# Graph layer on one core: edge lists loaded in runs of seven tiles, cast between the layer-norm groups

## The chip, the cores and the metric

The kernel runs on one core of a Trainium2 chip. A core has a matrix engine (TensorE, PE in the profile; PEld is its weight load), a vector engine (VectorE, DVE), a scalar engine (ScalarE, ACT), GpSimd (POOL) and a synchronisation engine (SyncE, SP) that here only issues DMAs. ACT and POOL issue DMAs as well. Every engine works through its own instructions in order, and waits on semaphores for the others. DMAs issued by SP, ACT and POOL go into separate queues (q1, q10 and q0 in the profile) which are served by the same 16 DMA engines. The metric is the time of one execution on the device in microseconds, less is better; the time before is a median of three runs.

## The reference

One graph layer over 6250 nodes of 256 features and 100000 edges, all in float32:

```
xn = layernorm(x)                                     # per node
x  = x + gnn(xn, src, dst) + mix(xn)
x  = x + lstm(layernorm(x))

gnn: neigh = segment_sum(xn[src], dst, N)             # dst is sorted
     h = relu(((1 + eps) * xn + neigh) @ W1 + b1) @ W2 + b2
     h = batchnorm over the nodes(h) * gamma + beta
mix: linear attention of 8 heads over all nodes, then an MLP with gelu, plus xn
lstm: one LSTM over the 6250 nodes in sequence, 256 wide, then two weighted running sums
```

`src` and `dst` are int32. The host pads both to 782 tiles of 128 edges (src with 0, dst with N = 6250) and hands them over as one flat run.

## The kernel before

**Layout.** The nodes lie as 125 rows ("c") by 50 steps ("s"), node = 50 c + s, with c on the partitions: `xn` is a tile of [125 of 128, 50, 256], and a DMA of n steps moves for each partition one run of n x 1024 bytes. `move` (L130) cuts every such DMA into two, partitions 0 to 111 and 112 to 124. `xnT` is the same transposed (features on the partitions), kept in the memory of `xr`.

**The head.** Six groups of steps (`LN_GROUPS`: 10, 10, 10, 10, 5, 5) are loaded by SP (L229), so twelve DMAs. Behind them on SP stand six small loads of `dst` in rows of 1024 edges (L230 to L235, tile `dg`), whose minima and maxima per 512 edges DVE takes at L317; at L329 it takes the same of runs of 256 edges for the first 34 groups. Those six go into `late`, the last ten steps of `xr`. ACT issues the load of a small table `vec` (L106) and then those of the edge lists themselves: src and dst each as 6 x 128 rows of 512 bytes (one row is one tile of 128 edges) and one DMA of the last 14 rows (L219, L220), into a corner of the tile `counts`. A tile of edges must end up as a column, an edge on each partition, because the gathers and selections of the later loop read columns. So L245 to L255 cast both lists to float32 on ACT (also in `late`), transpose 128 x 128 blocks on PE and copy them from PSUM to `si` (the sources as int32) and `drel` (the targets as float32).

The order on PE, DVE and ACT is written out by hand (`manual_schedule`); SP and POOL are ordered by the framework. Written order on these three: first the casts and transposes of both lists; then for each group `moments_of` (L270: statistics on DVE, one square root on ACT), in between DVE's operations the pending work of the group before (five small DVE operations and `normalise`, L287: scales two fifths of the rows on ACT, three fifths on POOL, and then issues the two writes of these steps to `xn_d` in DRAM on SP), then `columns_until` (L260): transposes of normalised steps on PE and copies to `xnT` on ACT, one group behind. After the last group come its normalisation, the reductions over `dg` and `flat`, and the remaining columns (L331), since these overwrite `late`. Then the loads of weights follow on SP: `w_qkv` into `m1` (L333), g1, g2, and the layer-norm table, w1 and w2 into `m2` (L336 to L339).

**Semaphores of DMAs.** The DMAs of SP and ACT share eight completion semaphores, given out in turn. A DMA that gets one that was used before waits on its issuing engine until that earlier DMA has landed. In the trace the order of handing out is `vec`, the first x load, the four edge loads, the other eleven x loads, the six `dg` loads, the twelve writes of `xn_d`, the weights.

**The rest.** Every gather (L372, POOL) fetches 128 rows of `xn_d` by a column of `si`, and can begin when all of `xn_d` is written. In a loop over 162 groups of four tiles, PE multiplies the rows by selections made from `drel` (L393) and DVE adds the result to `sums` (L403); the attention, the MLP, the counts of the first 34 groups and the node MLP (L574, L585) are interleaved with that by slots. The LSTM follows (L1042 to L1207), and a last pass adds and stores (L1288 to L1297).

Of the kernel before, what the change touches and what calls it, by code (L numbers as in the profile page):

```python
# [14 lines left out]
F32 = mybir.dt.float32  # L15
I32 = mybir.dt.int32
BF16 = mybir.dt.bfloat16
AF = mybir.ActivationFunctionType
# [5 lines left out]
P = 128  # L24
N, D, E = 6250, 256, 100000


NC, NS = 125, 50
HEADS, HC = 8, 32
KD = D // P  # L30
NE = -(-E // P)


GT, W = 4, 96
GROUPS = -(-NE // GT)
GE = GT * P
# [30 lines left out]
LN_GROUPS = [(0, 10), (10, 10), (20, 10), (30, 10), (40, 5), (45, 5)]  # L67
BANK = 512
# [22 lines left out]
def gps_layer(ctx: ExitStack, tc: tile.TileContext, x, src, dst, cols, rows, kvln, wqkv, mw1, mw2, gw1, gw2,  # L91
              wih, whh, blstm, out):
    nc = tc.nc
# [7 lines left out]
    ident = big.tile([P, P], F32, name="ident")  # L101
    make_identity(nc, ident)
    ones = big.tile([P, P], F32, name="ones")
# [34 lines left out]
    xr = big.tile([P, NS, D], F32, name="xr", tag="B")  # L138
    xnT = xr[:, :, :KD * NC].rearrange("p s (k c) -> p s k c", k=KD)

    m1 = big.tile([P, 2 * BANK * KD], F32, name="m1", tag="M1")
    w_qkv = m1[:, :KD * 3 * D].rearrange("p (k m) -> p k m", k=KD)
    kv_bias = m1[:, KD * 3 * D:]
    m2 = big.tile([P, 2 * BANK * KD], F32, name="m2", tag="M2")
# [11 lines left out]
    with ExitStack() as s1:  # L156
        wp = s1.enter_context(tc.tile_pool(name="wp", bufs=1))


        def edges_flat(t, start, ap):  # L160
            return bass.AP(tensor=t.tensor, offset=t.offset + start, ap=ap)

        si = wp.tile([P, NE], I32, name="si")
        base_i = wp.tile([1, GROUPS], I32, name="base_i")
        drel = wp.tile([P, NE], F32, name="drel")
        within = wp.tile([1, 1], I32, name="within")
        c_base = wp.tile([1, PAIRS], I32, name="c_base")
        g1 = wp.tile([P, KD, 2 * D], F32, name="g1")
# [6 lines left out]
        ope = wp.tile([P, 1], F32, name="ope")  # L175
# [14 lines left out]
        behind = place_x[:, at_x:]  # L190
# [13 lines left out]
        def from_bases(to, of, base_b, op):  # L204

            whole = NE // GT
            nc.vector.tensor_tensor(to[:, :whole * GT].rearrange("p (g t) -> p g t", t=GT),
                                    of[:, :whole * GT].rearrange("p (g t) -> p g t", t=GT),
                                    base_b[:, :whole, None].to_broadcast([P, whole, GT]), op=op)
            nc.vector.tensor_tensor(to[:, whole * GT:], of[:, whole * GT:],  # L210
                                    base_b[:, whole:].to_broadcast([P, NE - whole * GT]), op=op)

        with tc.tile_pool(name="ln1", bufs=2) as lp, tc.tile_pool(name="ps0", bufs=6, space=PSUM) as ps:
            FULL = NE // P
            late = xr.rearrange("p s d -> p (s d)")[:, (NS - 10) * D:]
            tiled = []
            for i, t in enumerate((src, dst)):
                s = behind[:, i * (FULL + 1) * P:(i + 1) * (FULL + 1) * P].bitcast(I32).rearrange("p (b e) -> p b e", e=P)
                nc.scalar.dma_start(s[:, :FULL, :], edges_flat(t, 0, [[P, P], [P * P, FULL], [1, P]]))  # L219
                nc.scalar.dma_start(s[:NE % P, FULL, :], edges_flat(t, FULL * P * P, [[P, NE % P], [1, P]]))  # L220
                tiled.append(s)

            rows_g = GROUPS // 2
            real = E - (rows_g - 1) * 2 * GE
            last = E - (GROUPS - 1) * GE
            flat = late[:, :2 * GE].bitcast(I32)
            dg = flat.rearrange("p (j e) -> p j e", j=2)
            for s0, n in LN_GROUPS:
                move(nc.sync, xn[:, s0:s0 + n, :], by_step(x)[:, s0:s0 + n, :])  # L229
# [3 lines left out]
            for at in range(real, 2 * GE, last):  # L233
                n = min(last, 2 * GE - at)
# [6 lines left out]
            nc.gpsimd.memset(counts, 0.0)  # L241

            with tc.manual_schedule(engines={mybir.EngineType.PE, mybir.EngineType.DVE, mybir.EngineType.Activation}):

                for s, to in zip(tiled, (si, drel)):  # L245
                    f = late[:, 2 * GE:2 * GE + (FULL + 1) * P].rearrange("p (b e) -> p b e", e=P)
                    nc.scalar.copy(f[:, :FULL, :], s[:, :FULL, :])
                    nc.scalar.copy(f[:NE % P, FULL, :], s[:NE % P, FULL, :])
                    for b0 in range(0, FULL + 1, 4):
                        pt = ps.tile([P, BANK], F32, name="mm")  # L250
                        w = min(NE - b0 * P, BANK)
                        for b in range(b0, min(b0 + 4, FULL + 1)):
                            r = min(P, NE - b * P)
                            nc.tensor.transpose(pt[:, (b - b0) * P:(b - b0) * P + r], f[:r, b, :], ident[:r, :r])
                        nc.scalar.copy(to[:, b0 * P:b0 * P + w], pt[:, :w])  # L255


                chunks = list(CHUNKS)
# [1 line left out]
                def columns_until(end):  # L260
                    while chunks and sum(chunks[0]) <= end:
                        s0, n = chunks.pop(0)
                        for k in range(KD):
                            pt = ps.tile([P, BANK], F32, name="mm")
                            for i in range(n):
                                nc.tensor.transpose(pt[:, i * NC:(i + 1) * NC], xn[:NC, s0 + i, k * P:(k + 1) * P],
                                                    ident[:NC, :NC])
                            nc.scalar.copy(xnT[:, s0:s0 + n, k, :], pt[:, :n * NC].rearrange("p (s c) -> p s c", c=NC))
# [33 lines left out]
                            partial(nc.vector.tensor_mul, rs, r, s), normalise]  # L302

                beside, done = [], 0
                for s0, n in LN_GROUPS:
                    more = moments_of(s0, n, beside)
                    while beside:
                        beside.pop(0)()
                    columns_until(done)
                    beside, done = more, s0  # L310
                for work in beside:
                    work()


                rows_c, each = COUNTED // 2, 2 * GT // CT
# [5 lines left out]
                for j in range(2):  # L321
                    b = ends[:rows_g, 0, j:j + 1]
                    pb = ps.tile([P, BANK], F32, name="mm")
                    nc.tensor.transpose(pb[:, :rows_g], b.to_broadcast([rows_g, P]), ident[:rows_g, :rows_g])
                    nc.vector.tensor_copy(base_b.rearrange("p (q j) -> p q j", j=2)[:, :, j], pb[:, :rows_g])
                    nc.vector.tensor_copy(base_i.rearrange("p (q j) -> p q j", j=2)[:, :, j], pb[:1, :rows_g])
                from_bases(drel, drel, base_b, ALU.subtract)
                for i, op in enumerate((ALU.min, ALU.max)):
                    nc.vector.tensor_reduce(pairs[:rows_c, i, :], flat[:rows_c, :].rearrange("p (j e) -> p j e", j=each),  # L329
# [31 lines left out]
        to = [sums[:, k, :N].rearrange("p (c s) -> p s c", s=NS) for k in range(KD)]  # L361
# [472 lines left out]
        with tc.If(held < GROUPS + PAIRS):  # L834
# [12 lines left out]
            base_b = mix_p.tile([P, 2 * D], F32, name="base_b", tag="t", bufs=4)  # L847
            nc.vector.tensor_copy(base_b[:, :GROUPS], pm[:, :GROUPS])
            from_bases(drel, drel, base_b[:, :GROUPS], ALU.add)
            with tc.For_i(0, NE, 1) as c:  # L850
                at = edge_p.tile([P, 1], I32, name="at1")
                nc.vector.tensor_copy(at, si[:, ds(c, 1)])
                d = edge_p.tile([P, 1], F32, name="d1")
                nc.vector.tensor_copy(d, drel[:, ds(c, 1)])
                g = gather(at[:, :1])
                for n0 in range(0, N + W, W):
                    w = min(W, N + W - n0)
# [14 lines left out]
        late = LATE / NS  # L872
# [71 lines left out]
    def summed(s, pool, pl):  # L944

        w = pool.tile([P, KD, NC], F32, name="w")
        nc.vector.scalar_tensor_tensor(w, pl[:, None, :].to_broadcast([P, KD, NC]), thr, of_step(s), op0=ALU.is_gt,
                                       op1=ALU.mult)
        if s == 0:
            nc.vector.tensor_copy(inc, w)  # L950
        else:
            nc.vector.tensor_add(inc, inc, w)
        for k in range(KD):
            weighted(s, 2, inc, k)
        return w
# [20 lines left out]
    with tc.tile_pool(name="lstm", bufs=2) as rp:  # L976
# [117 lines left out]
        with tc.manual_schedule(engines={mybir.EngineType.PE, mybir.EngineType.DVE, mybir.EngineType.Activation}):  # L1094
# [16 lines left out]
            for k in range(KD):  # L1111
                d = wl.tile([P, 1], F32, name="wlin_d")
# [57 lines left out]
        with tc.manual_schedule(engines={mybir.EngineType.PE, mybir.EngineType.DVE, mybir.EngineType.Activation}):  # L1170
            t = fetched.pop(0)
# [4 lines left out]
            w = None  # L1176
            for s in range(KEPT, NS):
                more = s + 1 < NS
                t = fetched.pop(0) if more else None
# [27 lines left out]
                w = summed(s - 1, rp, pl)  # L1207
# [9 lines left out]
        for i, (end, begin) in enumerate(((h, begin_h), (c, begin_c))):  # L1217
            d = rp.tile([P, KD, NC], F32, name="d", tag="h_w")[:, :, :NC - 1]
# [66 lines left out]
    with tc.tile_pool(name="post", bufs=3) as pp, tc.tile_pool(name="ps4", bufs=6, space=PSUM) as ps:  # L1285
        for i, (s0, n) in enumerate(CHUNKS):
# [4 lines left out]
            for s in range(s0, s0 + n):  # L1291
                pt = ps.tile([P, D], F32, name="pt")
# [66 lines left out]
```

## Time and profile before

| | |
|---|---|
| median of 3 runs (lowest, highest) | 1691.46 us (1687.46, 1699.31) |
| the profiled execution, its span | 1705.72 us, 1703.9 us |
| busy PE, DVE, ACT, POOL over the span | 86%, 55%, 39%, 41% |
| first gather | 62.97 us |
| products of the gathered rows (L393) | 70.1 to 1055.3 us |
| LSTM (L1042 to L1167) | 1077.8 to 1651.2 us |
| last pass (L1294) | from 1668.6 us |

The head in stretches of 5 us, from the table by stretches (busy us and, in brackets, instructions of each engine; then granted TensorE clock, mean busy share of the 16 DMA engines, and what they moved):

```profile
core 0: us, PE busy (x) PEld busy (x) DVE busy (x) ACT busy (x) POOL busy (x), PEclk, DMA share, GB/s
5.00:10.00 5.00, 0.00 (x0) 0.00 (x0) 1.14 (x6) 1.28 (x1) 5.00 (x1) 1.00 1.05 242
10.00:15.00 5.00, 0.00 (x0) 0.00 (x0) 3.14 (x18) 0.73 (x1) 0.48 (x2) 1.00 1.17 242
20.00:25.00 5.00, 0.00 (x0) 0.00 (x0) 0.00 (x0) 0.00 (x0) 0.00 (x0) 1.00 1.00 232
25.00:27.00 2.00, 0.00 (x0) 0.00 (x0) 0.00 (x0) 0.58 (x1) 0.00 (x0) 1.00 0.10 24
37.00:42.00 5.00, 3.76 (x17) 3.01 (x16) 4.96 (x29) 3.64 (x9) 3.26 (x6) 1.00 0.78 254
52.00:57.00 5.00, 2.55 (x23) 2.12 (x22) 4.49 (x14) 5.00 (x12) 2.54 (x5) 1.00 1.01 286
```

Up to 25 us the DMA engines are full while the four compute engines are nearly idle; from 25 to 27 us the DMA engines stand still too. From 37 us DVE has no idle time and paces the writes of `xn_d`.

### The profile page before, as it was taken

What the parts mean: (1) busy time and instruction counts of PE and PEld (TensorE: products, weight loads), DVE (VectorE), ACT (ScalarE), POOL (GpSimd) and SP (SyncE); (2) the same over time, 40 slices, a digit from 0 to 9 for tenths busy, and PEclk for the clock granted to TensorE, in tenths of its full rate; (3) what the DMA queues carried; (4) which work ended last, traced back from release to release, by engine and by line L of the source; (5) the groups of instructions that cost most, each with busy time, mean ns of one, the idle gap of its engine ahead of it and who ended that gap; (6) DMA issues with size and microseconds to landing.
All of it is one profiled execution on the core that took longest, in us unless ns stands there. A gap on an engine that the chain in (4) does not pass through costs nothing. (4 is left out here: it accounts for less than half of the span.)

```text
span 1703.9 us, 30469 instructions
## 1 busy us (share of the span) xinstructions
PE 1463.6 (86%) x11064; PEld 1383.9 (81%) x11064; DVE 938.7 (55%) x2931; ACT 659.7 (39%) x1921; POOL 694.1 (41%) x745
## 2 busy tenths in 40 slices
PE   2578888898888888988888888799999999999975
PEld 2567778787778888887888878799999999888874
DVE  3777677777773122212221222566667655788887
ACT  3532333333330122222222222566666643566650
POOL 3566666666666666666566663000010000000005
PEclk9789989999997999999999999899999999999997
DMA  8733323232334344433333333211111100233314
GB/s 212 232 85 89 89 86 88 84 89 84 89 88 137 116 128 130 125 107 101 92 102 102 102 99 106 86 62 74 62 74 67 68 38 2 73 110 109 110 50 152
DMA packets 64955, 165.98 MB, mean 97 GB/s; under 512 B 14409, under 2 KB 29499, under 8 KB 63792
## 3 DMA queue, kind: packets, MB, share of 16 engines
q0 software_dynamic: 31008, 84.71, 17.5%
q1 hardware_dynamic: 32016, 78.37, 14.3%
q8 instruction: 91, 1.49, 0.4%
q10 hardware_dynamic: 1768, 0.81, 0.2%
q14 instruction: 72, 0.59, 0.1%
HBM read 130.56 MB, written 33.28 MB: 96 GB/s over the span
## 5 line engine op out<-in xcount | busy, mean ns | idle before, releaser
L372 POOL DMA_INDIRECT eg<-xn_d,si x646 | 617.7, 956 | 376.1 <-PE pg L393 137.0
L393 PE MATMUL pg<-here,eg 128*128 128x96 f32 x2584 | 411.9, 286 | 34.5 <-issue 18.7
L393 PEld LDWEIGHTS pg<-here,eg 128*128 128x128 f32 x2584 | 383.8, 206 | 57.9 <-issue 43.8
L403 DVE TENSOR_TENSOR sums<-sums,pg 128x192 f32 x162 | 57.5, 355 | 494.8 <-PE pg L393 236.5
L1042 PE MATMUL pg<-yT,w_ih 128*128 128x125 f32 x1600 | 188.7, 276 | 0.7 <-ACT yT L1033 0.7
L1042 PEld LDWEIGHTS pg<-yT,w_ih 128*128 128x128 f32 x1600 | 184.3, 193 | 1.3 <-ACT yT L1033 1.3
L574 PE MATMUL mm<-sums,g 128*128 128x125 f32 x800 | 130.2, 300 | 33.5 <-issue 16.7
L590 ACT ACTIVATE sums<-mm,vec 128x125 f32<-128x125 f32 x100 | 36.4, 365 | 294.2 <-DVE sums L403 108.8
L574 PEld LDWEIGHTS mm<-sums,g 128*128 128x128 f32 x800 | 113.5, 210 | 42.6 <-issue 29.3
L1008 POOL TENSOR_TENSOR ln_r<-ln_v,minus_half 125x1 f32<-125x1 f32 x50 | 27.2, 548 | 291.3 <-DVE ln_v L1002 291.3
L1066 PE MATMUL pg<-h_w,w_hh 128*128 128x125 f32 x1248 | 145.7, 275 | 0.0
L1066 PEld LDWEIGHTS pg<-h_w,w_hh 128*128 128x128 f32 x1248 | 142.5, 192 | 0.0
L1288 POOL TENSOR_TENSOR xr<-xr,rest_t 125x1024 f32<-125x1024 f32 x8 | 23.0, 2906 | 278.7 <-DVEq L1233 278.7
L1075 ACT ACTIVATE gates<-pg,b_l 128x125 f32<-128x125 f32 x398 | 111.5, 362 | 56.9 <-PE pg L1066 35.7
L585 PE MATMUL mm<-z,g 128*128 128x125 f32 x800 | 119.9, 284 | 12.1 <-issue 10.7
L1167 PE MATMUL pg<-sums,w_hh 128*128 128x125 f32 x960 | 126.8, 275 | 0.0
L418 PE MATMUL mm<-m,xr 128*125 128x256 f32 x400 | 114.9, 415 | 12.8 <-DVE counts L613 8.9
L1167 PEld LDWEIGHTS pg<-sums,w_hh 128*128 128x128 f32 x960 | 116.8, 192 | 0.0
L585 PEld LDWEIGHTS mm<-z,g 128*128 128x128 f32 x800 | 104.1, 196 | 13.6 <-issue 12.0
L426 ACT ACTIVATE mm<-kv 125x512 f32<-125x512 f32 x50 | 30.1, 601 | 212.9 <-DVE kv L423 148.1
L580 ACT ACTIVATE z<-mm,vec 128x125 f32<-128x125 f32 x200 | 56.3, 366 | 114.9 <-PE pg L393 49.5
L418 PEld LDWEIGHTS mm<-m,xr 128*125 128x125 f32 x400 | 76.8, 207 | 23.5 <-issue 7.4
(273 smaller groups left out, 2369.4 us busy)
## 6 DMA issues: line engine op xcount, KB each, us to landing
x_d<-x_out SPq DMA_DIRECT2D x40, 500.0 KB
x_in<-x_d SPq DMA_DIRECT2D x40, 500.0 KB
eg<-xn_d,si POOLq DMA_INDIRECT x646
counts<-xn_d SPq DMA_DIRECT2D x16, 384.0 KB
m<-in_x_dram SPq DMA_DIRECT2D x50, 112.0 KB
out_dram<-o SPq DMA_DIRECT2D x12, 448.0 KB
xn<-in_x_dram SPq DMA_DIRECT2D x4, 1120.0 KB
xn_d<-xn SPq DMA_DIRECT2D x4, 1120.0 KB
```

The source lines that it names most:

```text
L372: nc.gpsimd.indirect_dma_start(out=g, out_offset=None, in_=xn_d[:], in_offset=bass.IndirectOffsetOnAxis(ap=at, axis=0))
L393: nc.tensor.matmul(pg[:, k, :], g[:, k * P:(k + 1) * P], here[:, i, :], start=(i == 0 and k == 0), stop=(i == n - 1), skip_group_check=True)
L403: nc.vector.tensor_add(window, window, pg)
L418: nc.tensor.matmul(pkv[:r, at], xnT[:, j, k, :], w_qkv[:, k, D:][:, at], start=(k == 0 and half == 0), stop=(k == KD - 1), skip_group_chec ...
L574: nc.tensor.matmul(p1[:, m, :], g1[:, k, m * P:(m + 1) * P], sums[:, k, at], start=(m == 0 and k == 0), stop=(k == KD - 1), skip_group_che ...
L580: nc.scalar.activation(z1[:, m, :], p1[:, m, :], AF.Relu, bias=col("gb1", m))
L585: nc.tensor.matmul(p2[:, a, :], g2[:, m, a * P:(a + 1) * P], z1[:, m, :], start=(a == 0 and m == 0), stop=(m == 2 * KD - 1), skip_group_ch ...
L590: nc.scalar.activation(sums[:, a, at], p2[:, a, :], AF.Identity, bias=col("gb2", a))
L1042: nc.tensor.matmul(pg[:, SLOT[g], :], w_ih[:, k, block(g, a)], yT[:, k, s * NC:(s + 1) * NC], start=(i == 0 and k == 0), stop=False, skip_ ...
L1066: nc.tensor.matmul(banks[a][:, SLOT[g], :], w_hh[:, k, block(g, a)], h[:, k, :], start=False, stop=(k == KD - 1), skip_group_check=True)
L1075: nc.scalar.activation(gate[g], pg[:, SLOT[g], :], AF.Tanh if g == G else AF.Sigmoid, bias=bias(g, a))
L1167: nc.tensor.matmul(to, w_hh[:, k, block(g, a)], of_step(s - 1)[:, k, :], start=False, stop=(k == KD - 1), skip_group_check=True)
```

## The change

Each list is loaded as 112 rows of seven tiles (896 edges, 3584 bytes): 111 whole rows in one DMA, the last row's five tiles in a second one, and two tiles of padding (taken from the list's start, never used) in a third. A row is cast in one ACT instruction; the seven 112 x 128 blocks are transposed, and the copies out of PSUM put block j at every seventh column from j on, so that `si` and `drel` hold the same columns as before (they are two columns wider). The cast data lies in `m1` (the later `w_qkv`) instead of `late`, and the `dg` rows in `m2` (later w1 and w2). In the hand-written order the casts of src come after the moments of group 0 and those of dst after the moments and pending work of group 2, each ahead of that group's columns; a square root of ones goes first on ACT. In the last turn of the loop the columns are left out, and follow after the last group's normalisation.

```diff
@@ -160,9 +160,12 @@
         def edges_flat(t, start, ap):
             return bass.AP(tensor=t.tensor, offset=t.offset + start, ap=ap)
-        si = wp.tile([P, NE], I32, name="si")
+        EP = 7
+        rows_e = -(-NE // EP)
+        si = wp.tile([P, rows_e * EP], I32, name="si")
         base_i = wp.tile([1, GROUPS], I32, name="base_i")
-        drel = wp.tile([P, NE], F32, name="drel")
+        drel = wp.tile([P, rows_e * EP], F32, name="drel")
         within = wp.tile([1, 1], I32, name="within")
         c_base = wp.tile([1, PAIRS], I32, name="c_base")
         g1 = wp.tile([P, KD, 2 * D], F32, name="g1")
@@ -207,23 +210,26 @@
             nc.vector.tensor_tensor(to[:, :whole * GT].rearrange("p (g t) -> p g t", t=GT),
                                     of[:, :whole * GT].rearrange("p (g t) -> p g t", t=GT),
                                     base_b[:, :whole, None].to_broadcast([P, whole, GT]), op=op)
-            nc.vector.tensor_tensor(to[:, whole * GT:], of[:, whole * GT:],
+            nc.vector.tensor_tensor(to[:, whole * GT:NE], of[:, whole * GT:NE],
                                     base_b[:, whole:].to_broadcast([P, NE - whole * GT]), op=op)
         with tc.tile_pool(name="ln1", bufs=2) as lp, tc.tile_pool(name="ps0", bufs=6, space=PSUM) as ps:
-            FULL = NE // P
-            late = xr.rearrange("p s d -> p (s d)")[:, (NS - 10) * D:]
             tiled = []
+            left = NE - (rows_e - 1) * EP
             for i, t in enumerate((src, dst)):
-                s = behind[:, i * (FULL + 1) * P:(i + 1) * (FULL + 1) * P].bitcast(I32).rearrange("p (b e) -> p b e", e=P)
-                nc.scalar.dma_start(s[:, :FULL, :], edges_flat(t, 0, [[P, P], [P * P, FULL], [1, P]]))
-                nc.scalar.dma_start(s[:NE % P, FULL, :], edges_flat(t, FULL * P * P, [[P, NE % P], [1, P]]))
+                s = behind[:, i * EP * P:(i + 1) * EP * P].bitcast(I32)
+                nc.scalar.dma_start(s[:rows_e - 1], edges_flat(t, 0, [[EP * P, rows_e - 1], [1, EP * P]]))
+                nc.scalar.dma_start(s[rows_e - 1:rows_e, :left * P],
+                                    edges_flat(t, (rows_e - 1) * EP * P, [[left * P, 1], [1, left * P]]))
+                if left < EP:
+                    nc.scalar.dma_start(s[rows_e - 1:rows_e, left * P:], edges_flat(t, 0, [[P, 1], [1, (EP - left) * P]]))
                 tiled.append(s)
             rows_g = GROUPS // 2
             real = E - (rows_g - 1) * 2 * GE
             last = E - (GROUPS - 1) * GE
-            flat = late[:, :2 * GE].bitcast(I32)
+            flat = m2[:, :2 * GE].bitcast(I32)
             dg = flat.rearrange("p (j e) -> p j e", j=2)
             for s0, n in LN_GROUPS:
                 move(nc.sync, xn[:, s0:s0 + n, :], by_step(x)[:, s0:s0 + n, :])
@@ -241,18 +247,23 @@
             nc.gpsimd.memset(counts, 0.0)
             with tc.manual_schedule(engines={mybir.EngineType.PE, mybir.EngineType.DVE, mybir.EngineType.Activation}):
-                for s, to in zip(tiled, (si, drel)):
-                    f = late[:, 2 * GE:2 * GE + (FULL + 1) * P].rearrange("p (b e) -> p b e", e=P)
-                    nc.scalar.copy(f[:, :FULL, :], s[:, :FULL, :])
-                    nc.scalar.copy(f[:NE % P, FULL, :], s[:NE % P, FULL, :])
-                    for b0 in range(0, FULL + 1, 4):
+                def edges_to_partitions(i):
+                    to = (si, drel)[i].rearrange("p (q j) -> p j q", j=EP)
+                    f = m1[:, i * EP * P:(i + 1) * EP * P]
+                    nc.scalar.copy(f[:rows_e], tiled[i][:rows_e])
+                    for j0 in range(0, EP, 4):
+                        n = min(4, EP - j0)
                         pt = ps.tile([P, BANK], F32, name="mm")
-                        w = min(NE - b0 * P, BANK)
-                        for b in range(b0, min(b0 + 4, FULL + 1)):
-                            r = min(P, NE - b * P)
-                            nc.tensor.transpose(pt[:, (b - b0) * P:(b - b0) * P + r], f[:r, b, :], ident[:r, :r])
-                        nc.scalar.copy(to[:, b0 * P:b0 * P + w], pt[:, :w])
+                        pt = pt[:, :n * rows_e].rearrange("p (j q) -> p j q", q=rows_e)
+                        for j in range(n):
+                            nc.tensor.transpose(pt[:, j, :], f[:rows_e, (j0 + j) * P:(j0 + j + 1) * P],
+                                                ident[:rows_e, :rows_e])
+                        nc.scalar.copy(to[:, j0:j0 + n, :], pt)
+                nc.scalar.activation(ope, ones[:, 0:1], AF.Sqrt)
                 chunks = list(CHUNKS)
@@ -302,14 +313,18 @@
                             partial(nc.vector.tensor_mul, rs, r, s), normalise]
                 beside, done = [], 0
-                for s0, n in LN_GROUPS:
+                for i, (s0, n) in enumerate(LN_GROUPS):
                     more = moments_of(s0, n, beside)
                     while beside:
                         beside.pop(0)()
-                    columns_until(done)
+                    if i in (0, 2):
+                        edges_to_partitions(i // 2)
+                    if i < len(LN_GROUPS) - 1:
+                        columns_until(done)
                     beside, done = more, s0
                 for work in beside:
                     work()
+                columns_until(done)
                 rows_c, each = COUNTED // 2, 2 * GT // CT
```

## The prediction

> **What bounds the kernel now.** I read the page first, then three stretches of the trace.
>
> ```profile
> PE   2578888898888888988888888799999999999975
> DMA  8733323232334344433333333211111100233314
> L372 POOL DMA_INDIRECT eg<-xn_d,si x646 | 617.7, 956 | 376.1 <-PE pg L393 137.0
> ```
>
> From the third slice on (a slice is 42.6 us) TensorE is busy to eight or nine tenths and POOL's gathers mostly wait for it: the gather loop and the LSTM are TensorE's. Only the first slice and a half is different: PE 2 and 5, DMA 8. The change lies wholly there. The page's chain of waits covers only the last 35 us, so I asked the head directly. Its end is the first gather, which needs every row of `xn_d`:
>
> ```profile
> 36.93 21.43 SPq L133 DMA_DIRECT2D xn_d<-xn  x12
> 62.97 1.19 POOL L372 DMA_INDIRECT eg<-xn_d,si  x1 [7.51 <-ACT xr L268]
> 70.09 7.31 PE L393 MATMUL pg<-here,eg 128*128 128x96 f32 x32 [12.13 <-DMA eg<-xn_d,si]
> ```
>
> The twelve writes of `xn_d` leave from 36.93 us; the last landing on their queue comes at 61.95, then the last column copies of ACT (to 62.83) hold POOL 0.9 us more. Whatever moves 62.97 moves everything behind it by as much. Why do the writes start at 36.93? The waits up to 36 us on the SP queue, and the timeline of ACT:
>
> ```profile
> SPq L133 <- DMA counts<-in_dst_dram: 11.2, 1, 11.2
> SPq L133 <- DMA vec<-in_cols_dram: 6.7, 1, 6.7
> SPq L133 <- DMA counts<-in_src_dram: 5.1, 2, 4.9
> ```
>
> ```profile
> 14.27 0.83 ACT L247 CAST xr<-counts 128x768 f32<-128x768 int32 x1 [4.45 <-DMA counts<-in_src_dram]
> 26.42 0.83 ACT L247 CAST xr<-counts 128x768 f32<-128x768 int32 x1 [9.03 <-DMA counts<-in_dst_dram]
> 30.79 0.21 ACT L284 ACTIVATE ln_s<-ln_v 125x10 f32<-125x10 f32 x1
> ```
>
> The edges delay two things. ACT can't take the first square root before both arrays are cast: it was ready at 13.2 (the end of L283) and runs at 30.79. And the loads of `x`, which have no use for edges, wait for them too: a load reuses the completion semaphore of the eighth DMA before it, so SP, which goes in order, stands before the loads from step 20 on until src and then dst have landed.
>
> **How edges and x share the engines.** The DMA queue view of 8.4 to 11.2 us (q1 is SP's queue, q10 ACT's):
>
> ```profile
> q1 hardware_dynamic: 74, 0.76, 99.0%
> q10 hardware_dynamic: 81, 0.04, 7.1%
> ```
>
> With both queues full an engine takes about one packet of each in turn, 74 against 81. An x packet (10,240 B) costs 0.99 x 2.8 us x 16 / 74 = 0.60 us of an engine, an edge packet (512 B) 0.039. From 52 to 54 us, where nothing but writes moves, 60 packets in 99.1% of 2 us make 0.53 us each.
>
> **The change, part by part.**
>
> **Edge loads.** Two of 768 packets and two of 14 become, for each array, one of 111 rows of 3,584 B, one row of 2,560 and one of 1,024. What decides is over how many engines 111 rows are spread. The trace has a neighbour: the last load of L720, 106 rows of 1,024 B, against a load of 3 x 128 rows of the same line (719.4 to 723.2 us, then 736.2 to 740.5):
>
> ```profile
> q1 hardware_dynamic: 400, 0.39, 36.6%
> ...
> q1 hardware_dynamic: 108, 0.11, 9.7%
> ```
>
> 400 packets are 384 of data and 16 completions; 108 are 106 and 2. So 106 rows ran on two engines, at 0.097 x 4.3 x 16 / 108 = 0.062 us a packet, and took as long as the whole 384 KB. The Trainium skill (DMA: Bandwidth & Descriptors, "Why a DMA increments its semaphore by 16 and not by 1") has the rule: the largest count up to 16 that divides the outer dimension of both sides. 106 gives 2, as seen; 112 and 128 give 16; 111 = 3 x 37 gives 3. No run here shows 111. By the rule each edge array is 37 packets on each of three engines, which carry a sixteenth of x each as well; by an even spread (as the 14-row load had 14) it is 7 on sixteen. The first is my main sum, the second the first rival.
>
> A packet of 3,584 B: the floor is the fastest stretch of the trace, 376 GB/s from 63 to 66 us, 23.5 B/ns an engine: 0.153 us (and 0.436 for an x packet). At the loaded x rate it is 0.21 (0.60), at seven 512 B packets 0.275. Since thirteen engines are idle for part of the time I take the middle of the first two, 0.18 and 0.52.
>
> **Sum for the three slow engines.** src starts behind `vec` at about 7 us: 37 x 0.18 + 8 x packets x 0.52 = 10.9, done at 17.9, landed 19.1 with 1.2 us for a completion (before: 14.3). SP then sends the next three x loads, 9 packets on such an engine: 37 x 0.18 + 9 x 0.52 = 11.4, so dst is done at 29.3, landed 30.5 (before: 26.4). With six edge loads instead of four in the ring of eight, steps 30 to 49 are behind dst: 8 x 0.60 + 16 x 0.30 (rows of 5,120 B) = 9.6, plus 1.2 to start and 1.2 to land: x is in at 42.5, against 34.4 before. SP issues in order, and the writes of `xn_d` reuse semaphores of the last x loads, so they start at 42.5 instead of 36.93. They are no longer paced by the statistics (4.78 us a group), only by the engines: 40 packets x 0.53 = 21.2, plus 2.4, end 66.1. That is 4.1 later; the 0.9 of column copies is gone (they are done long before): **+3.2 us**.
>
> **Casts behind the first scales.** The same fourteen transposes and four PSUM copies; one cast of 112x896 an array (0.97 by 0.83 for 768) for 0.83 + 0.29. On ACT, src now stands ahead of the group 0 normalisation and the second root, dst ahead of the third group's and the first columns. Queued behind these waits: ACT's normalisations, DVE's reciprocals, and through them the writes, all ready before SP is free at 42.5. If that cover went (the even spread), both arrays land by 15 us and hold nobody. A table load of 1.28 us may fall away or move: free, ACT is not late. The additional square root is one 0.2 us instruction in ACT's idle start.
>
> **Last rows ahead of the columns.** The last x at 42.5 + 2.8 (five moments) + about 4 for root, scale and normalisation is 49; the writes that go first last until about 62. Worth nothing here; the order before cost up to 3 us, as the last ACT normalisation ran at 57.0, 6.5 us after the last moments.
>
> **Staging.** `w_qkv` now waits for the transposes of the edges (about 33 us, load due after 58: hidden). The loads into `m2` wait for the reductions L317 to L329, 6.3 us that end near 56, due near 63: hidden by 7 us. POOL's memset and iotas stay; its normalisations follow the groups. The two padding columns are not read.
>
> All differences are made against the profiled execution: 1703.9 span, 1705.72 in all, 14 above the median 1691.46 of the runs. I carry the difference to the median: 1691.5 + 3 = **1694.5**.
>
> **The rivals.**
> 1. *Even spread, or x not held up.* On sixteen engines an edge array costs 7 x 0.21 = 1.5 us. An engine has 24 for x, 3 for edges, 1.5 for the dst groups from 1.7 us: x in at 31.5, writes 23.6 more, 55.1; 6.9 + 0.9 = 7.8 earlier: 1683.5. For it: the DMA hole at 25 to 27 us (24 GB/s) and ACT's 9 us wait disappear. Against it: the 106 rows.
> 2. *Slower than before: row price.* If a 3,584 B row costs what seven 512 B packets do (0.275) with x at 0.60, src lands at 23.2, dst at 38.8, x at 50.8, the writes at 74.4: +12.4 - 0.9 = 11.5, 1703. With x at 0.52 the change turns to a loss from 74 rows x 0.138 us on; the middle case is past that by little. Against it: 1,024 B packets cost 0.062, which makes 0.22.
> 3. *The loop answers.* A later start shifts the warm-up of the TensorE clock (0.50 from 63 to 80 us); PE would stand idle some 5 us longer before it. I see no lever for more than a few us.
>
> **How the numbers follow.** Main case 0.50 (bounds of its costs: -0.5 to +6.7, so 1691 to 1698), rival 1 0.23, rival 2 0.20, the rest 0.07. The runs before scatter by 0.35% to each side, so 1% (17 us) is about what can be told from no change. No case reaches it by itself: more than 17 slower is the upper end of rival 2 with scatter, or the loop, 0.11; more than 17 faster is rival 1 with scatter, 0.09; within 0.80. The range takes in the centres of rivals 1 and 2: 1682 to 1704.
>
> **What would show it.** Right: edge loads landing near 19 and 30 us, SP waiting for dst longer than 11 us, the first `xn_d` write after 40 with writes back to back, first gather near 66. Wrong: dst in by 15, first write near 31, gather near 55 (rival 1); first gather after 70 (rival 2); or a gather time that moves while the end doesn't follow.

## The result, and the profile after

| | before | after |
|---|---|---|
| median of 20 runs each (lowest, highest) | 1693.34 us (1687.46, 1699.43) | 1700.06 us (1692.29, 1708.29) |
| ratio, 95% interval | 1 | 1.0037 (1.0025 to 1.0048) |
| profiled execution, its span | 1705.72, 1703.9 us | 1693.55, 1691.8 us |
| src, dst landed | 14.3, 26.3 us | 17.8, 30.6 us |
| x landed, first write of `xn_d` issued | 34.8, 36.93 us | 44.3, 44.19 us |
| last write landed, first gather | 61.92, 62.97 us | 68.9, 70.05 us |
| first and last product of the gathered rows | 70.1, 1055.3 us | 76.0, 1043.3 us |

The change costs 6.7 us, 0.4%. The two profiled executions have it the other way round: the span of after is 12 us shorter although its head is 7 us longer. The difference lies in the gather loop, which took 985 us in the one execution and 967 us in the other, the same code in both. The 20 runs of one kernel also lie 12 to 16 us apart, more than the whole effect, so the total is judged by their medians, and the profiles are used for what the change touches, the head.

The page of after, the 40 slices: the first two of PE are 1 and 4 (before 2 and 5), those of DMA 7 and 8 (before 8 and 7). Less is done early; the rest is as it was.

```profile
PE   1479888888898889988888987899999999999975
...
DMA  7833333323334344433333333211111100233314
```

The waits of the SP queue in the first 45 us of after (total us, times, longest us), and what SP issues until 80 us (start, us from the first to the last of the group):

```profile
SPq L133 <- DMA counts<-in_dst_dram: 11.6, 1, 11.6
SPq L133 <- DMA counts<-in_src_dram: 9.5, 1, 9.5
```

```profile
0.73 32.53 SPq L133 DMA_DIRECT2D xn<-in_x_dram  x12
...
44.19 20.49 SPq L133 DMA_DIRECT2D xn_d<-xn  x12
```

SP stands 9.5 us for src and 11.6 us for dst, which its loads of `x` don't use; the twelve loads of `x` take until 33.3 us to issue. The writes begin at 44.19, as the last of `x` comes in, and leave back to back. The timelines of ACT, POOL and PE:

```profile
18.32 0.94 ACT L255 CAST m<-counts 112x896 f32<-112x896 int32 x1 [5.11 <-DMA xn<-in_x_dram]
29.60 2.07 ACT L304 ACTIVATE xn<-xn,ln_shift,ln_rs 125x256 f32<-125x256 f32 x4 [7.63 <-DVE ln_shift L299]
36.46 0.92 ACT L255 CAST m<-counts 112x896 f32<-112x896 int32 x1
```

```profile
70.05 1.19 POOL L387 DMA_INDIRECT eg<-xn_d,si  x1 [15.35 <-DMA m<-in_wqkv_dram]
76.00 6.82 PE L408 MATMUL pg<-here,eg 128*128 128x96 f32 x32 [17.12 <-DMA eg<-xn_d,si]
```

Group 0 is normalised from 29.6 although its `x` landed by 8.6: its pending work is written between DVE's statistics of the next group, and those wait for `x`. Two of the names in brackets mislead, because several DMAs share a semaphore. What the first cast waits for is src, whose last piece landed at 18.21. And the weight load named behind the gather lands at 70.85, after the gather has left. The gather leaves 1.18 us after the last write of `xn_d` has landed (68.87), and it does so in every changed kernel below except e2; in e2 and in before it is 1.06 us. So the last write releases it.

How many engines carry the edges shows in stretches where the other engines have nothing left to do. Two rows of the queue view of after for 14 to 17 us (packets, MB, mean share of 16 engines), then the table by stretches of 8 to 44 us (columns as in the table before):

```profile
q1 hardware_dynamic: 20, 0.15, 12.4%
...
q10 hardware_dynamic: 18, 0.06, 5.3%
```

```profile
8.00:14.00 6.00, 0.00 (x0) 0.00 (x0) 4.28 (x21) 1.70 (x3) 2.49 (x2) 1.00 0.84 212
14.00:18.00 4.00, 0.00 (x0) 0.00 (x0) 0.00 (x0) 0.00 (x0) 0.00 (x0) 1.00 0.18 73
18.00:26.00 8.00, 1.54 (x7) 1.22 (x7) 0.00 (x0) 2.49 (x3) 0.00 (x0) 1.00 0.88 185
26.00:31.00 5.00, 0.00 (x0) 0.00 (x0) 4.27 (x25) 1.40 (x3) 1.33 (x3) 1.00 0.14 54
31.00:44.00 13.00, 6.56 (x46) 6.56 (x47) 10.30 (x59) 8.97 (x19) 7.78 (x15) 1.00 0.95 227
```

17.7% of sixteen engines is 2.8: three are busy and thirteen stand still, from 14 to 18 us until src is in and again from 26 to 31 until dst is. The single packets of that stretch come in threes: three edge rows (0.14 us each), then three `x` packets (0.39 us each), in turn. The trace also has three landing events for each load of 111 rows, 16 for one of 112 rows, two for one of 106.

### The profile page after: what moved, and what is told of

The parts are those of the page before. It is cut to its first block, busy times and chain, and to the rows that moved or that the text cites. A ratio compares the mean times of both kernels' runs of the same rounds, so it can differ in the third digit from the quotient of the medians.

```text
span 1691.8 us, 30463 instructions
## 1 busy us (share of the span) xinstructions
PE 1451.5 (86%) x11064; PEld 1377.2 (81%) x11064; DVE 939.4 (56%) x2931; ACT 660.8 (39%) x1919; POOL 695.7 (41%) x745
## 5 line engine op out<-in xcount | busy, mean ns | idle before, releaser
L408 PE MATMUL pg<-here,eg 128*128 128x96 f32 x2584 | 409.4, 286 | 35.2 <-DMA eg<-xn_d,si 17.1
L1057 PE MATMUL pg<-yT,w_ih 128*128 128x125 f32 x1600 | 188.6, 276 | 0.7 <-ACT yT L1048 0.7
L1090 ACT ACTIVATE gates<-pg,b_l 128x125 f32<-128x125 f32 x398 | 111.8, 363 | 56.3 <-PE pg L1081 35.4
L600 PE MATMUL mm<-z,g 128*128 128x125 f32 x800 | 116.4, 282 | 4.5 <-issue 3.7
L433 PEld LDWEIGHTS mm<-m,xr 128*125 128x125 f32 x400 | 78.0, 211 | 23.5 <-issue 11.3
```

The source lines that it names most:

```text
L408: nc.tensor.matmul(pg[:, k, :], g[:, k * P:(k + 1) * P], here[:, i, :], start=(i == 0 and k == 0), stop=(i == n - 1), skip_group_check=True)
L433: nc.tensor.matmul(pkv[:r, at], xnT[:, j, k, :], w_qkv[:, k, D:][:, at], start=(k == 0 and half == 0), stop=(k == KD - 1), skip_group_chec ...
L600: nc.tensor.matmul(p2[:, a, :], g2[:, m, a * P:(a + 1) * P], z1[:, m, :], start=(a == 0 and m == 0), stop=(m == 2 * KD - 1), skip_group_ch ...
L1057: nc.tensor.matmul(pg[:, SLOT[g], :], w_ih[:, k, block(g, a)], yT[:, k, s * NC:(s + 1) * NC], start=(i == 0 and k == 0), stop=False, skip_ ...
L1090: nc.scalar.activation(gate[g], pg[:, SLOT[g], :], AF.Tanh if g == G else AF.Sigmoid, bias=bias(g, a))
```

## The experiments

Two theories. **A, three engines:** 111 rows run on three engines; they delay src and dst, and with them, through the shared semaphores, `x`, the writes and the gathers. **B, the order:** the casts behind the first scales, or the new staging, hold ACT and DVE and so the writes. The experiments ran on three chips: on that of e1 to e4 the kernel before took 1545.88 us, on that of e5 to e7 1693.77 us, on that of e8 1546.4 us. So totals are given as ratios to the kernel before on the same chip. Which chip the pair of before and after ran on is not on record; by its time it is of the slower sort. The first column of times is for the largest load of each list; its last row comes up to 4.7 us later.

| kernel | src, dst landed | x landed | first write | first gather | ratio, 95% interval |
|---|---|---|---|---|---|
| before | 14.3, 26.3 | 34.8 | 36.93 | 62.97 | 1 |
| after | 17.8, 30.6 | 44.3 | 44.19 | 70.05 | 1.0037 (1.0025 to 1.0048) |
| e1_even | 9.8, 11.4 | 33.7 | 33.51 | 60.82 | 0.9971 (0.9960 to 0.9981) |
| e2_short_rows | 13.6, 26.0 | 35.4 | 35.23 | 60.30 | 0.9970 (0.9958 to 0.9981) |
| e3_casts_first | 17.7, 30.4 | 43.9 | 43.59 | 68.51 | 1.0046 (1.0028 to 1.0064) |
| e4_first_even | 10.0, 11.7 | 34.1 | 34.02 | 59.57 | 0.9968 (0.9957 to 0.9979) |
| e5_even_last | 31.7, 33.3 | 30.3 | 33.62 | 59.28 | 0.9986 (0.9975 to 0.9998) |
| e6_one_engine | 29.1, 54.0 | 62.3 | 61.93 | 87.05 | 1.0136 (1.0115 to 1.0158) |
| e7_three_last | 34.5, 39.9 | 29.3 | 40.24 | 66.11 | 1.0027 (1.0017 to 1.0037) |
| e8_writes_early | 9.9, 11.4 | 33.8 | 23.71 | 56.14 | 0.9940 (0.9919 to 0.9961) |

**e1_even: the same rows over more engines.** 96 and 15 rows in place of 111, the padding cleared by DVE instead of loaded, so still three loads for an array (two big and the last row).

```diff
+                nc.vector.memset(s[96:rows_e, left * P:], 0)
-                nc.scalar.dma_start(s[:rows_e - 1], edges_flat(t, 0, [[EP * P, rows_e - 1], [1, EP * P]]))
+                nc.scalar.dma_start(s[:96], edges_flat(t, 0, [[EP * P, 96], [1, EP * P]]))
+                nc.scalar.dma_start(s[96:rows_e - 1], edges_flat(t, 96 * EP * P, [[EP * P, rows_e - 1 - 96], [1, EP * P]]))
...
-                if left < EP:
-                    nc.scalar.dma_start(s[rows_e - 1:rows_e, left * P:], edges_flat(t, 0, [[P, 1], [1, (EP - left) * P]]))
```

> The changed kernel, but the 111 rows of each edge list go in two DMAs of 96 and 15 rows (16 and 15 engines) and the two padding tiles are cleared on VectorE in place of their load, so that six edge loads stay. Theory A (111 rows run on three engines, which hold up src, dst and by the shared semaphores the loads of x): src lands by 11, dst by 15 us, x is in near 32, first gather at 55 to 58, ratio to the kernel before 0.993 to 0.997. Theory B (the written order and the new staging cost the time, the loads don't matter): first gather stays near 70, ratio near 1.0037.

The waits of SP, the first writes and the first gather of e1, and its table by the same stretches:

```profile
SPq L133 <- DMA counts<-in_dst_dram: 2.7, 1, 2.7
SPq L133 <- DMA counts<-in_src_dram: 1.5, 1, 1.5
```

```profile
33.51 21.78 SPq L133 DMA_DIRECT2D xn_d<-xn  x12
...
60.82 1.19 POOL L387 DMA_INDIRECT eg<-xn_d,si  x1 [15.13 <-DMA m<-in_wqkv_dram]
```

```profile
8.00:14.00 6.00, 0.00 (x0) 0.00 (x0) 4.28 (x21) 2.24 (x4) 2.49 (x2) 1.00 1.05 272
14.00:18.00 4.00, 1.54 (x7) 1.22 (x7) 0.71 (x3) 1.84 (x3) 0.00 (x0) 1.00 1.04 233
18.00:26.00 8.00, 0.00 (x0) 0.00 (x0) 7.31 (x45) 2.59 (x6) 3.59 (x7) 1.00 1.01 242
26.00:31.00 5.00, 2.36 (x12) 2.36 (x13) 4.04 (x23) 3.90 (x8) 2.90 (x6) 1.00 0.97 226
31.00:44.00 13.00, 9.59 (x77) 8.34 (x75) 9.36 (x53) 12.20 (x29) 8.12 (x15) 1.00 0.90 269
```

The two idle stretches are gone. Length times DMA share, summed over the five rows, is 25.9 us of work for all sixteen engines in after and 35.1 us here: 9.2 us more done by 44 us, and the first gather is 9.2 us earlier. The sign of the change turns with the number of rows in a load; the one other difference, two small padding loads that became clears on DVE, was not tried alone. The gather itself was expected at 55 to 58 and came at 60.8: `x` was in at 33.7 instead of 32, and the writes took 26 us from the first issue to the last landing. They could have begun earlier:

```profile
20.23 3.25 POOL L306 TENSOR_SCALAR xn<-xn,ln_rs,ln_shift 125x256 f32<-125x256 f32 x6 [9.74 <-DVE ln_shift L299]
28.34 3.08 SPq L241 DMA_DIRECT2D m<-in_dst_dram  x3
```

Group 0 is normalised at 23.5, but its write stands on SP behind the `dg` loads, the last of which leave from 28.34 to 31.4. e8 moves these.

**e2_short_rows: the loads of before in the new places.** The 512-byte loads, two casts and the copies of before are put into `edges_to_partitions`; the staging in `m1` and `m2`, the casts behind the first scales and the last columns stay as the change has them.

```diff
-                nc.scalar.dma_start(s[:rows_e - 1], edges_flat(t, 0, [[EP * P, rows_e - 1], [1, EP * P]]))
...
+                nc.scalar.dma_start(s[:, :FULL, :], edges_flat(t, 0, [[P, P], [P * P, FULL], [1, P]]))
+                nc.scalar.dma_start(s[:NE % P, FULL, :], edges_flat(t, FULL * P * P, [[P, NE % P], [1, P]]))
...
+                    nc.scalar.copy(f[:, :FULL, :], s[:, :FULL, :])
+                    nc.scalar.copy(f[:NE % P, FULL, :], s[:NE % P, FULL, :])
```

> The changed kernel with the edge loads, casts and transposes in the form of before (rows of 512 bytes), but at the new place in the order and with the new staging. Theory A: dst lands near 26 as before, x in near 34, first gather 60 to 63, ratio 0.997 to 1.000. Theory B: first gather near 70, ratio near 1.0037.

```profile
13.18 0.21 ACT L292 ACTIVATE ln_s<-ln_v 125x10 f32<-125x10 f32 x1 [3.00 <-DVE ln_v L291]
35.23 19.61 SPq L133 DMA_DIRECT2D xn_d<-xn  x12
```

0.9970: with the old loads the rest of the change is a gain of 0.3%. Theory B, for which it should be slower than before, falls. dst still lands at 26.0 and `x` at 35.4, close to before; the writes start 1.7 us earlier and the last of them lands at 59.2 instead of 61.92. With the first root at 13.18 instead of 30.79 the groups are normalised ahead. The writes of the first four leave at 35.2, 36.3, 39.0 and 44.9 us, where in before they left at 36.9, 41.7, 46.5 and 51.1, held by DVE's statistics (DVE busy 4.96 of each 5 us up to 47, 3.95 in the next five).

**e3_casts_first, e4_first_even: the order undone.** Both casts go ahead of the first root again, in e3 with the loads of the change, in e4 with those of e1.

```diff
+                edges_to_partitions(0)
+                edges_to_partitions(1)
                 nc.scalar.activation(ope, ones[:, 0:1], AF.Sqrt)
...
-                    if i in (0, 2):
-                        edges_to_partitions(i // 2)
```

> The changed kernel with its long rows on three engines, but both casts put back in front of the first square root. Theory A: dst still lands near 30.6, the first root comes near 35, the writes are paced by VectorE from there: first gather 68 to 72, ratio 1.003 to 1.005, so the order is worth next to nothing with these loads. Theory B: first gather near 63, ratio near 1.000.

> Casts in front as in e3, but 96 and 15 rows as in e1. Theory A: dst lands by 15, the first root near 19, x in near 32: first gather 56 to 60, ratio 0.994 to 0.998, within 2 us of e1. Theory B: first gather near 63, ratio near 1.000.

The first lines are of e3, where the first root of ACT stands behind dst, as in before; the others are the first root of e4 and the first gathers of e3 and e4:

```profile
31.33 0.94 ACT L255 CAST m<-counts 112x896 f32<-112x896 int32 x1 [8.25 <-DMA counts<-in_dst_dram]
...
36.33 0.19 ACT L297 ACTIVATE ln_s<-ln_v 125x10 f32<-125x10 f32 x1
```

```profile
21.40 0.20 ACT L297 ACTIVATE ln_s<-ln_v 125x10 f32<-125x10 f32 x1
```

```profile
68.51 1.19 POOL L387 DMA_INDIRECT eg<-xn_d,si  x1 [7.53 <-issue]
59.57 1.19 POOL L387 DMA_INDIRECT eg<-xn_d,si  x1 [13.51 <-DMA m<-in_wqkv_dram]
```

e3 and e4 are the cleanest pair for theory A: one chip, the same order, and only the rows (with the padding) differ. 1.0046 becomes 0.9968, and the first gather comes 8.9 us earlier.

The root of e3 is 23 us later than in after (12.99 us), and the writes start 0.6 us earlier than there: with three engines ACT's order is hidden by `x`, which comes at 44 in both. The ratios, 1.0046 against 1.0037, can't be told apart, nor can e4's 0.9968 and e1's 0.9971. So the order alone is worth nothing measurable with either of these loads. Before has neither even rows nor the later casts; e4 has the one, e2 the other, e1 both, and all three gain the same 4 to 5 us. That fits two remedies for one wait, the late first root. But the new staging and the last columns stand in all three as well, and no run takes these out, so their share is not shown.

**e5_even_last, e7_three_last: edges behind x.** The edge loads go to SP behind all loads of `x`, so that `x` waits for no edge, and the casts stand beside the last two groups. e5 has the rows of e1, e7 those of the change.

```diff
-                nc.scalar.dma_start(s[:rows_e - 1], edges_flat(t, 0, [[EP * P, rows_e - 1], [1, EP * P]]))
...
                 move(nc.sync, xn[:, s0:s0 + n, :], by_step(x)[:, s0:s0 + n, :])
...
+                nc.sync.dma_start(s[:rows_e - 1], edges_flat(t, 0, [[EP * P, rows_e - 1], [1, EP * P]]))
...
-                    if i in (0, 2):
-                        edges_to_partitions(i // 2)
+                    if i >= 4:
+                        edges_to_partitions(i - 4)
```

> Edge loads of 96 and 15 rows as in e1, but issued by SP behind all loads of x (so no load of x waits for edges), and cast beside the last two groups. Theory A (what counts is when x is in and the writes of xn_d can start): x in by 28 us, the first write near 29, first gather at 55 to 57 against 60.8 in e1, ratio to before 0.992 to 0.995, faster than e1 by 0.2 to 0.4%. If the writes are instead held by the edge loads that now stand before them on SP, first gather stays at 59 to 61 and the ratio at 0.997.

> The changed kernel's own loads of 111 rows, issued by SP behind all loads of x as in e5. It takes apart the two ways in which the long rows delay x: the shared semaphores (gone here) and the load on three engines (still there, now before the writes). Theory A: x in by 28 us; the three engines carry 74 x 0.15 = 11 us of rows before their share of the writes, so the first gather comes at 62 to 66, ratio 0.999 to 1.002: about half of what the change loses against e5 is the semaphores, half the engines. If only the semaphores count: first gather near 56, ratio as e5. If only the engines count: near 70, ratio near 1.0037.

The first write and the first gather of e5, then of e7:

```profile
33.62 20.61 SPq L133 DMA_DIRECT2D xn_d<-xn  x12
...
59.28 1.19 POOL L386 DMA_INDIRECT eg<-xn_d,si  x1 [15.77 <-DMA m<-in_wqkv_dram]
```

```profile
40.24 20.78 SPq L133 DMA_DIRECT2D xn_d<-xn  x12
...
66.11 1.19 POOL L386 DMA_INDIRECT eg<-xn_d,si  x1 [22.05 <-DMA m<-in_wqkv_dram]
```

`x` is in at 30.3 and 29.3. In e5 group 0 is ready long before its write:

```profile
17.16 3.26 POOL L305 TENSOR_SCALAR xn<-xn,ln_rs,ln_shift 125x256 f32<-125x256 f32 x6 [6.67 <-DVE ln_shift L298]
```

Normalised at 20.4, written at 33.62: SP issues in order, and the edge and `dg` loads ahead of it wait for semaphores. Here the alternative named in the expectation came, and the ratio, 0.9986, gains less than e1 (0.9971), though the intervals overlap. In e7 three engines carry the edges after `x`, so the writes start at 40.24, 6.6 us later than in e5, and 102 GB/s are moved from 30 to 40 us (245 in e5). The three first gathers, 59.28 (e5), 66.11 (e7) and 70.05 (after), divide the cost: 6.8 us for three engines instead of sixteen with `x` out of the way, 3.9 us more for the place in which the loads also hold `x`. The second figure is rough, since in after the casts stand elsewhere too. e7's gather and ratio (1.0027) lie just above what was expected; taking the loads out of the way of `x` doesn't save the change.

**e6_one_engine: the dose.** e1 with 109 for 96: 109 is a prime, and two rows follow.

```diff
-                nc.scalar.dma_start(s[:96], edges_flat(t, 0, [[EP * P, 96], [1, EP * P]]))
+                nc.scalar.dma_start(s[:109], edges_flat(t, 0, [[EP * P, 109], [1, EP * P]]))
```

> The changed kernel with each list's rows in two DMAs of 109 and 2 rows (109 is prime, so one engine), the padding cleared on VectorE. Theory A: src lands near 27, dst near 46, x is in near 60, first gather at 84 to 88, ratio 1.012 to 1.018. If the number of engines doesn't matter, it stays near 1.0037 with the first gather near 70.

The queue view of e6 for 20 to 28 us, its writes and the first gather:

```profile
q10 hardware_dynamic: 56, 0.20, 6.4%
```

```profile
61.93 19.59 SPq L133 DMA_DIRECT2D xn_d<-xn  x12
...
87.05 1.19 POOL L387 DMA_INDIRECT eg<-xn_d,si  x1 [13.99 <-DMA m<-in_wqkv_dram]
```

One sixteenth is 6.25%: one engine is busy, and for eight microseconds nothing else moves. First gathers at 60.8 (16 and 15 engines), 70.05 (three) and 87.05 (one), ratios 0.9971, 1.0037 and 1.0136; both numbers of e6 lie where A put them, though dst landed at 54.0, not near 46: ACT stood for 14.7 us in its issue of the two-row load of src and sent the 109 rows of dst only at 16.72. Its first root waited for these issues too (43.39 us), but the writes start only as the last of `x` comes in (62.3). e6 and e1 differ in nothing but the rows (and the chip), so theory A is shown by the dose, not only by the removal.

**e8_writes_early: a version that beats both.** What is left in e1 is SP's order. So the `dg` loads follow the writes of the third group. The program text also puts the src loads behind two groups of `x` and the dst loads behind three.

```diff
-            for i, t in enumerate((src, dst)):
+            def load_edges(i, t):
...
+            for j, (s0, n) in enumerate(LN_GROUPS):
                 move(nc.sync, xn[:, s0:s0 + n, :], by_step(x)[:, s0:s0 + n, :])
+                if j in (1, 2):
+                    load_edges(j - 1, (src, dst)[j - 1])
...
                         move(nc.sync, by_step(xn_d)[:, s0:s0 + n, :], xn[:, s0:s0 + n, :])
+                        if s0 == 20:
+                            load_targets()
```

> A version meant to beat both: even edge loads (96 and 15 rows), those of src issued by ACT behind two groups of x, those of dst behind three; the six loads of dst rows for the minima move on SP from behind x to behind the writes of the third group, so that the first write of xn_d can go as soon as its group is normalised. Theory A: an engine has 24 us of x, 3 of edges, 1.5 of dst rows and 21 of writes from 1.7 us, so with no hole the last write lands near 53: first write near 20, first gather at 54 to 57, ratio 0.992 to 0.996. If the writes can't run beside the loads without slowing them, or the semaphores hold them, first gather stays at 59 to 61 and the ratio at 0.997.

```profile
23.71 13.87 SPq L133 DMA_DIRECT2D xn_d<-xn  x6
37.63 2.04 SPq L231 DMA_DIRECT2D m<-in_dst_dram  x1
...
44.17 6.94 SPq L133 DMA_DIRECT2D xn_d<-xn  x6
...
56.14 1.19 POOL L394 DMA_INDIRECT eg<-xn_d,si  x1 [10.10 <-issue]
```

These are lines of SP's and POOL's timeline of e8. Half of the writes leave between 23.7 and 37.6 us, beside the last of `x`, and the first gather comes 6.8 us before that of the kernel before. 1536.91 against 1546.4 us, ratio 0.9940: faster than both kernels. The loads of the edges did not move. ACT sends them in e1 (first line) and in e8 (second line) at the same time:

```profile
2.63 0.34 ACTq L223 DMA_DIRECT2D counts<-in_dst_dram  x1
```

```profile
2.64 0.32 ACTq L224 DMA_DIRECT2D counts<-in_dst_dram  x1
```

src and dst land at 9.9 and 11.4 us (9.8 and 11.4 in e1), and `x` at 33.8 (33.7). So what e8 gains over e1 in the head, 4.7 us at the first gather, comes from the place of the `dg` loads alone.

Over all nine changed kernels the total follows the first gather to within 2.7 us; among the four kernels from -2.2 to -3.7 us it does not order them. Its shift against 62.97, with the difference of the medians to the kernel before behind it, is in us: e8 -6.8, -9.5; e5 -3.7, -2.2; e4 -3.4, -4.4; e2 -2.7, -5.0; e1 -2.2, -4.0; e7 +3.1, +4.0; e3 +5.5, +6.5 (by its medians of 1552.35 and 1545.88); after +7.1, +6.7; e6 +24.1, +22.1. (The 62.97 is of one profile, on a chip of the slower sort; no profile of the kernel before was kept from the faster ones.)

## Why the prediction was right

Foretold was 3 us more than before, from the three engines; it is 6.7 us more, from the three engines. What was off is the size: the 6.7 us lie at the upper end of the main case (-0.5 to +6.7). That the total fell into the range, 1682 to 1704, says little, since the range took in the centres of both rivals; the landing times decide.

**The step that decides, the number of engines: right.** 111 rows went over three engines (three landing events), as foretold; the first rival, an even spread, is what e1 had to build. The rival's time, 7.8 us earlier than before, wasn't reached by that alone: e1 gains 4.0 us, and 9.5 us only came with e8's later `dg` loads.

**The sum for the three engines: right, in part by luck.** From the start of src to the end of dst it gave 22.3 us; measured are 22.4 (7 us to 30.61 less 1.2 for a completion). Two errors cancel in it: src landed at 17.8, 1.3 us before the sum, and dst landed 12.8 us behind src, where the sum had 11.4. A row of 3584 bytes was put at 0.18 us throughout. While the other thirteen engines stood still it took 0.14 (18 packets in 5.3% of 3 us on 16 engines), and alone in e6 0.146 (56 packets in 6.4% of 8 us); the mean of all 222 rows in the trace of after is 0.21. The second rival, a row at 0.275 throughout, would have src at 23.2. Its sign, a first gather after 70, did come by a hair (70.05), but not its landings.

**Everything that follows from the wait: right in kind, short by 3.9 us at the gather.** The last landing was put at 66.1 and the first gather near 66; the gather came at 70.05. Three terms of the sum were mis-sized. The last loads of `x` behind dst were put at 12.0 us and took 13.7 (30.6 to 44.3). The writes, with their start and landing, were put at 23.6 us and took 24.7 (44.19 to 68.87). And the 0.9 us of the column copies did not come back: the gather leaves 1.18 us after the last write has landed, in before 1.06 us after it, so that hold never was a separate one. 1.7 + 1.1 + 0.9 make 3.7 of the 3.9; the end moved by 6.7 us instead of 3.

**The edits costed at nothing: right.** Moving the casts behind the scales is hidden as long as `x` comes last (e3). Staging and columns cost nothing that shows: e2, which has all of them, is faster than before. What the prediction didn't see is that the edits together are worth 5 us in e2, where no load of 111 rows covers them.

**The third rival, the loop:** no sign of it. The median moved by 6.7 us, the gather by 7.1.

## What to carry to other kernels

In these traces the number of rows of a load decides how many engines carry it: by their landing events 112 and 96 rows went over 16 engines, 15 over 15, 111 over three and 109 over one. Before making rows longer to have fewer packets, count what the row count divides by, and split an awkward one (111 = 96 + 15). A slow load can hold loads that have nothing to do with it, by a shared semaphore or by an in-order queue: look in the waits of the issuing queue for names that its own work doesn't need. And a change of several parts can hide a gain under a loss: run the parts apart before throwing it away.

## What the hardware showed unexpectedly

An issue can itself last long. In e6 ACT's issue of the two-row load behind the 109 rows on one engine took 14.7 us for src and 24.6 us for dst; the longest issue of an edge load took 2.7 us in after and 5.6 us in before. That the loaded engine holds the issue is likely, but no run shows it.

The same kernel before took 1693.77 us on one chip, 1545.88 and 1546.4 us on two others. The LSTM's multiplications by `w_ih` were busy 188.6 us in after, on a chip of the slower sort, and 190.0 us in e1 on a faster one; the gather loop took 967 us in the one and 824 us in the other, at a mean granted clock over the span of 0.939 and 0.964. No run here was made to find why.
